# One causal convolution layer on a Trainium2 core: the input projection as seven block products instead of eight, with its sums on VectorE and a short convolution spread over three engines

## The chip, the core and the metric

The kernel runs on one core of a Trainium2 chip, in fp32 throughout. Time is device time in microseconds of one launch. Its engines are called here by what the profile calls them: PE (TensorE, the matrix engine), DVE (VectorE), ACT (ScalarE), POOL (GpSimd) and SP (the engine that issues most DMAs). PE multiplies a stationary block of weights with moving columns and writes into PSUM, eight banks of 512 fp32 columns for 128 partitions; DVE, ACT and POOL work on SBUF, and DVE and ACT also read and write PSUM. Each engine takes its instructions in order and stands at one whose operands are not ready.

## The reference

The input is x of 8192 tokens by 512 channels. A layer of the kind "long convolution with gates" is followed by a mixture of 32 x 4 small experts; each is added to its input and normalized. What matters here is the beginning:

```python
u = x @ W_in + b_in                          # 8192 x 1536
uc = _short_conv(u, short_w, short_b)        # 3 taps along the tokens, per channel
x0, x1, v = jnp.split(uc, 3, axis=-1)
v = v * x1
k = _gen_filter(x.shape[1], W1, b1, f1, W2, b2, f2, W3, b3)   # two sine layers, then 512 channels
v = _causal_fft_conv(v, k, filter_bias)      # the long convolution
y = v * x0
return y @ W_out + b_out
```

The filter k depends on the position alone: a 3-row table goes through two dense layers with a sine each, a third layer to 512 channels, and a decay by an exponential.

## The kernel before

The program has stages that follow each other: `project`, `convolve` (the long convolution as matmuls with tables of cosines and sines), and `experts`. Only `project` is touched. It has channels on the partitions and tokens along the columns. Between the stages three arrays lie in DRAM: x0, the gate (v * x1) and the taps (the filter k).

**The projection.** Sixteen blocks of 512 tokens, and in each four tiles of 128 channels. `projection(b, ct)` forms the tile's three outputs s = 0, 1, 2 (x0, x1 and v), each from four matmuls over 128 of the 512 input channels (L260, fp32, 128x512), in a PSUM bank of its own. All PSUM banks of the stage come from one pool of eight single banks.

**The short convolution.** For each s, ACT moves the bank to SBUF with the bias (L269, into `u`, which has two columns more for the last two tokens of the block before), and multiplies by the third tap (L271). DVE adds the second tap (L272) and the first (L277, or L283 in two halves for s = 0, whose result is stored in another order). POOL copies the two last columns to `carry` and back (L253, L286) and multiplies the outputs 1 and 2 (L288). SP stores x0 and the gate (256 KB each).

**The filter, riding along.** `rides` is a list of 16 filter steps and 32 tap groups, dealt out over the 64 (b, ct) pairs in order: behind each pair the loop issues as many as fall due. A filter step (`filter_1` or `filter_2`) is one 128x512 matmul (L209, L215) and a `sine`: seven DVE instructions (L197 to L202: a reduction of the argument in three steps with `n` and `a`, then a clamp) and ACT's sine (L203). A tap group (`some_taps`) has eight short matmuls into two banks (`pk`); for each bank ACT makes four 128x128 exponentials `ex` (L238), DVE adds the bias to give `kb` (L241), and POOL multiplies the two into `taps` (L245). A finished tile of taps (4 MB) is stored by SP.

**Order.** Tiles come from pools with a number of buffers for each tag (`bufs`); a new tile of a tag waits until the oldest one's readers are done. A scheduler of the build orders the instructions on each engine, and the waits follow from reads, writes and buffers. Tokens come in as `xt`, 1 MB for a block, with two buffers.

## Time and profile before

| | before |
|---|---|
| median of 3 runs | 2326.41 us (2322.28 to 2327.26) |
| profiled execution | 2320.76 us, its span 2319.0 us |
| mean granted PE clock | 0.969 |
| PE busy in the span | 2152.6 us (93%) |
| DVE, ACT, POOL busy | 1297.3 (56%), 823.7 (36%), 478.2 us (21%) |
| the projection's matmuls (L260) | 1536 records, 673.5 us busy |
| waits in the span's first 724 us before L260 | 4.8 us |

The slices of the page cut the span in 40 equal parts of 58 us; a digit is the busy share in tenths. The groups give, for a line of the code, an engine and the names of what is written and read, the count, the busy time, the mean of one in ns, and the time that the engine stood idle just before, with what ended most of it. An fp32 matmul of 512 columns leaves two records and two weight loads in this trace. The first stage takes the first 724 us, some twelve and a half slices.

### The profile page before, as it was taken

To read this page: it belongs to the slowest core of one execution; us is meant where nothing else is said; L and a number is where in the kernel's file an instruction comes from. 1 tells how busy PE (TensorE), PEld (TensorE's weight loads), DVE (VectorE), ACT (ScalarE), POOL (GpSimd) and SP (SyncE) were. 2 spreads that over 40 slices of the span, in tenths; PEclk is the share of its full clock that TensorE was granted. 3 is DMA by queue.
4 is the path that set the end of the run, shared out by engine and by line. 5 is a ranking of instruction groups with operands and counts; after the bars stand their busy time and mean duration, and the time that the engine had idled before them with its cause. 6 is when DMAs were issued, how large, how long until landed. Compare 5 with 4: busy or idle time off the path is not lost. (4 is left out here: it accounts for less than half of the span.)

```text
span 2319.0 us, 65860 instructions
## 1 busy us (share of the span) xinstructions
PE 2152.6 (93%) x29664; PEld 1474.7 (64%) x29664; DVE 1297.3 (56%) x1872; ACT 823.7 (36%) x1248; POOL 478.2 (21%) x583
## 2 busy tenths in 40 slices
PE   9999999999999999999999998889988999888765
PEld 3444444444446999999999998355555556555643
DVE  5677544554544553463463463456566666656647
ACT  4444555555553321231321221121343234224433
POOL 1111333333331340250250160211100100110000
PEclk9999999999999999999999999999998999899887
DMA  5222224232414655655564574526654754665373
GB/s 167 68 64 76 70 65 167 87 136 64 141 59 168 204 172 192 194 199 183 184 219 174 165 245 167 154 77 195 216 193 136 230 185 137 194 217 188 118 264 121
DMA packets 197057, 362.62 MB, mean 156 GB/s; under 512 B 79132, under 2 KB 118946, under 8 KB 193698
## 3 DMA queue, kind: packets, MB, share of 16 engines
q1 hardware_dynamic: 194472, 341.63, 45.2%
q10 hardware_dynamic: 2304, 16.78, 1.8%
q8 instruction: 233, 3.82, 0.7%
q14 instruction: 48, 0.39, 0.1%
HBM read 274.47 MB, written 83.89 MB: 155 GB/s over the span
## 5 line engine op out<-in xcount | busy, mean ns | idle before, releaser
L260 PE MATMUL pu<-xt,win 128*128 128x512 f32 x1536 | 673.5, 596 | 4.8 <-DMA xt<-in_xT 4.8
L260 PEld LDWEIGHTS pu<-xt,win 128*128 128x128 f32 x1536 | 289.2, 190 | 363.8 <-issue 355.0
L272 DVE SCALAR_TENSOR_TENSOR o<-u,chan_sb,o 128x512 f32<-128x512 f32 x192 | 144.8, 754 | 289.6 <-ACT o L271 270.6
L554 PE MATMUL po<-wout,yt 128*128 128x512 f32 x512 | 240.7, 614 | 19.4 <-DVE x L558 19.2
L383 PE MATMUL px<-place,tab 128*64 128x128 f32 x4096 | 227.6, 273 | 2.2 <-ACT place L366 1.4
L383 PEld LDWEIGHTS px<-place,tab 128*64 128x64 f32 x4096 | 226.0, 136 | 3.3 <-ACT place L366 2.1
L359 PE MATMUL pa<-c_in_sb,vk 128*64 128x128 f32 x4096 | 224.9, 273 | 2.3 <-ACT place L366 1.6
L359 PEld LDWEIGHTS pa<-c_in_sb,vk 128*64 128x64 f32 x4096 | 223.5, 137 | 3.9 <-ACT place L366 1.8
L552 POOL TENSOR_TENSOR xt<-xt,b_outb_sb 128x512 f32<-128x512 f32 x64 | 82.4, 1288 | 619.9 <-DMA xt<-in_x 581.1
L269 ACT ACTIVATE u<-pu,chan_sb 128x512 f32<-128x512 f32 x192 | 130.6, 680 | 182.8 <-PE pu L260 179.0
L405 POOL TENSOR_TENSOR place<-t,hs 128x256 f32<-128x256 f32 x132 | 94.8, 718 | 470.8 <-DVE hs L403 411.2
L554 PEld LDWEIGHTS po<-wout,yt 128*128 128x128 f32 x512 | 94.4, 194 | 130.1 <-issue 96.1
L717 ACT COPY si<-pi 128x1024 f32<-128x1024 f32 x96 | 93.0, 1012 | 196.6 <-PE pi L708 138.3
L271 ACT ACTIVATE o<-u,chan_sb 128x512 f32<-128x512 f32 x192 | 155.6, 812 | 6.5
L368 DVE COPY place<-pa 128x1024 f32<-128x1024 f32 x64 | 78.3, 1224 | 139.7 <-PE pa L359 135.1
L721 DVE STREAM_TRANSPOSE si<-si 128x2048 f32<-128x2048 f32 x48 | 108.1, 2290 | 85.0 <-ACT si L717 85.0
L366 ACT COPY place<-pa 128x1024 f32<-128x1024 f32 x64 | 64.7, 1012 | 251.8 <-PE pa L359 245.7
L416 PE MATMUL pz<-c_back_sb,place 64*128 64x128 f32 x2048 | 123.6, 284 | 14.8 <-POOL place L405 14.8
L238 ACT ACTIVATE ex<-delta_sb,negt_sb 128x128 f32<-128x128 f32 x256 | 87.6, 390 | 132.9 <-POOL taps L245 132.9
L416 PEld LDWEIGHTS pz<-c_back_sb,place 64*128 64x128 f32 x2048 | 122.8, 199 | 15.8 <-POOL place L405 15.8
L708 PE MATMUL pi<-f,h 32*32 32x128 f32 x6144 | 103.4, 291 | 30.2 <-issue 18.2
L398 ACT COPY hs<-px 128x512 f32<-128x512 f32 x132 | 75.5, 572 | 156.9 <-PE px L383 149.0
(86 smaller groups left out, 2655.9 us busy)
## 6 DMA issues: line engine op xcount, KB each, us to landing
f<-in_f SPq DMA_DIRECT2D x160, 512.0 KB, 5.1
tab<-in_c_mid SPq DMA_DIRECT2D x64, 512.0 KB, 3.8
place<-in_c_out SPq DMA_DIRECT2D x64, 512.0 KB, 5.0
x<-o SPq DMA_DIRECT2D x64, 256.0 KB, 2.4
gate<-gate SPq DMA_DIRECT2D x64, 256.0 KB, 2.6
taps<-taps SPq DMA_DIRECT2D x4, 4096.0 KB, 11.2
vk<-taps SPq DMA_DIRECT2D x32, 512.0 KB, 4.0
vk<-gate SPq DMA_DIRECT2D x32, 512.0 KB, 3.5
```

Source lines behind the costliest of these rows:

```text
L260: nc.tensor.matmul(pss[s], win[ct][:, k, s, :], xt[:, k, :], start=(k == 0), stop=(k == NCT - 1))
L269: nc.scalar.activation(u[:, s, 2:], pss[s], AF.Identity, bias=ch(0))
L271: nc.scalar.activation(o, u[:, s, 2:], AF.Identity, bias=ch(1), scale=ch(4))
L272: nc.vector.scalar_tensor_tensor(o, u[:, s, 1 : 1 + TB], ch(3), o, ALU.mult, ALU.add)
L359: nc.tensor.matmul(ps[r * 64 : (r + 1) * 64, c * N1 : (c + 1) * N1], vk[:, half * 8 + c, :], cin[:, r, :], start=True, stop=True,)
L383: nc.tensor.matmul(ps[h * 64 : (h + 1) * 64, j, :, r, :], tab[:, g % 2 * KC + j, r * 64 : (r + 1) * 64], both[:, :, g * KC + j, h * 64 : ( ...
L405: nc.gpsimd.tensor_tensor(o[:, 0], t[:, 0], hs[:, 1], ALU.subtract)
L416: nc.tensor.matmul(ps[:, h, c, :], spec[rows, r, c0 + c, :], cback[rows, r].rearrange("p q n -> p (q n)"), start=(r == 0), stop=(r == 1),)
L554: nc.tensor.matmul(ps, got["y"][:, ct, t % 2 * P : (t % 2 + 1) * P], wout[:, ct, :], start=(ct == 0), stop=(ct == NCT - 1),)
L708: nc.tensor.matmul(pss[r // 2][s * T : (s + 1) * T, col : col + P], b.h[rows, at + q, s, u * T : (u + 1) * T], f2[rows, q, s, :], start=Tr ...
L717: nc.scalar.copy(o, pss[rr].rearrange("p (r q d) -> p r d q", r=2, q=4))
L721: nc.vector.transpose(turned[:, d].rearrange("p d g -> p (d g)"), stage[:, d].rearrange("p d e -> p (d e)"),)
```

## The change

The projection takes double blocks of 1024 tokens and pairs of channel tiles m and m + 2, so that a "quad" (b, m, s) is a product of a 2 x 2 block matrix of weights (two channel tiles by two halves of the 512 input channels) with a 2 x 2 block matrix of tokens (two halves of the input channels by two runs of 512 tokens). Such a product takes eight block products when written out. The changed kernel forms it from seven, on sums of weight blocks and of token blocks. A block product is two fp32 128x512 matmuls (L317).

- *Sums of operands.* Four sums of weight blocks for each m at the start (L184 to L187, DVE for m = 0 and POOL for m = 1), and four differences of token tiles `t1` to `t4` for each double block (L208; on DVE for the first one, on POOL after that). `t1` has two buffers, the others one.
- *Sums of results.* p1 has a single bank and goes to SBUF by ACT (L327). The other six products fall in three bank pairs: p26, p75 and p43. DVE adds each pair of banks in one instruction of 1024 columns (L338, L350, L355), and once 512 columns (L351). The pairs come from a pool of two, so that p26 of a quad takes the pair that p75 of the quad before gives back, and so on in turn. The other four banks are a pool of single banks, for p1, the short convolution's halves (`o_`), the filter steps and the tap groups.
- *The short convolution* of a quad is issued in the middle of the next one: ACT multiplies by the first tap in SBUF (L372, 1024 columns) and by the third, with a combined bias, into a single PSUM bank (L379, 512 columns); DVE adds the second tap (L387, reads PSUM, writes SBUF); POOL adds the first (L397, or L401 for s = 0). For s = 1 quads after the first 27, DVE adds the first tap (L391) and ACT's part of it falls away. The bias of the projection enters by the combined bias; `carry` starts with minus the bias. POOL multiplies the gate (L411), 1024 columns at once.
- *Order.* PE's instructions keep the order in which they are written (`manual_schedule`); the other engines' are ordered by the scheduler. A quad has on PE: p1, p26, the rides that are due, p75, p43. The 16 filter steps fall in the first 27 quads, the 32 tap groups in the next 19. The outputs go in the order s = 1, 2, 0.
- *Loads.* The first weight block is loaded by ACT's queue. Tokens come as four tiles of 512 KB for a double block, from a tag with five buffers; the position rows for `filter_1` in eight loads.

The diff (empty lines left out):

```diff
--- before.py
+++ after.py
@@ -125,12 +125,18 @@
             for name in ("chan", "c_in", "c_back")
         }
         between = in_dram("x0", [P, L]), in_dram("gate", [P, P, N2]), in_dram("taps", [P, P, N2])
-        with tc.tile_pool(name="psum1", bufs=8, space=bass.MemoryType.PSUM) as psum:
+        with (
+            tc.tile_pool(name="psum1", bufs=4, space=bass.MemoryType.PSUM) as psum,
+            tc.tile_pool(name="psum0", bufs=2, space=bass.MemoryType.PSUM) as psum0,
+        ):
             def bank(name):
                 return psum.tile([P, 512], F32, tag="ps", name=name)
-            project(tc, i, bank, load, between, kept)
+            def pair(name):
+                return psum0.tile([P, 2, TB], F32, tag="pair", name=name)
+            project(tc, i, bank, pair, load, between, kept, pairs)
         with tc.tile_pool(
             name="psum2", bufs=4, space=bass.MemoryType.PSUM, reuse_waits="tile"
         ) as psum:
@@ -142,43 +148,80 @@
     experts(tc, i, load, ident, y_dram, out)
-def project(tc, i, bank, load, between, kept):
+def project(tc, i, bank, pair, load, between, kept, small):
     nc = tc.nc
     x0_dram, gate_dram, taps_dram = between
-    with tc.tile_pool(name="pr1", bufs=1) as hp, tc.tile_pool(name="pr2", bufs=2) as wk:
-        win = [hp.tile([P, NCT, 3, P], F32, tag=f"win{ct}", name=f"win{ct}") for ct in range(NCT)]
-        def load_win(ct):
+    with (
+        tc.tile_pool(name="pr1", bufs=1) as hp,
+        tc.tile_pool(name="pr2", bufs=2) as wk,
+        tc.manual_schedule(engines={nc.tensor.engine}),
+    ):
+        NP = NCT // 2
+        A11, A12, S3, A22, S1, S2, S4 = range(7)
+        win = [hp.tile([P, 7, 3, 2, P], F32, tag=f"win{m}", name=f"win{m}") for m in range(NP)]
+        def load_win(m, queue):
             come = i["W_in"].rearrange("(k p) (s t c) -> k t p s c", p=P, s=3, c=P)
+            for half in range(2):
+                for k in range(NCT):
+                    queue.dma_start(
+                        out=win[m][:, 2 * half + k // 2, :, k % 2, :], in_=come[k, m + NP * half]
+                    )
+        def sums_of_win(m, e):
+            w = win[m]
+            e.tensor_tensor(w[:, S1], w[:, S3], w[:, A22], ALU.add)
+            e.tensor_tensor(w[:, S2], w[:, S1], w[:, A11], ALU.subtract)
+            e.tensor_tensor(w[:, S4], w[:, A12], w[:, S2], ALU.subtract)
+            e.tensor_tensor(w[:, S3], w[:, A11], w[:, S3], ALU.subtract)
         def load_tokens(b):
-            xt = wk.tile([P, NCT, TB], F32, tag="xt", name=f"xt_{b}")
-            nc.sync.dma_start(
-                out=xt, in_=i["xT"][:, b * TB : (b + 1) * TB].rearrange("(k p) t -> p k t", p=P)
+            got = {}
+            for name, h, n in (("12", 0, 1), ("11", 0, 0), ("21", 1, 0), ("22", 1, 1)):
+                got[name] = xq = wk.tile([P, 2, TB], F32, tag="xq", name=f"xq{name}_{b}", bufs=5)
+                t0 = (2 * b + n) * TB
+                nc.sync.dma_start(
+                    out=xq,
+                    in_=i["xT"][2 * h * P : 2 * (h + 1) * P, t0 : t0 + TB].rearrange(
+                        "(k p) t -> p k t", p=P
+                    ),
+                )
+            return got
+        def sum_of_tokens(b, x, name, e):
+            a, c = {"1": ("12", "11"), "2": ("22", "t1"), "3": ("22", "12"), "4": ("21", "t2")}[name]
+            x["t" + name] = t = wk.tile(
+                [P, 2, TB], F32, tag=f"xs{name}", name=f"xs{name}_{b}", bufs=2 if name == "1" else 1
             )
-            return xt
-        xt = wk.tile([P, NCT, TB], F32, tag="xt", name="xt_0")
-        for k in range(NCT):
-            nc.sync.dma_start(
-                out=win[0][:, k],
-                in_=i["W_in"].rearrange("(k p) (s t c) -> k t p s c", p=P, s=3, c=P)[k, 0],
-            )
-            nc.sync.dma_start(out=xt[:, k], in_=i["xT"][k * P : (k + 1) * P, 0:TB])
-        pe = load(hp, "pe")
+            e.tensor_tensor(t, x[a], x[c], ALU.subtract)
+        load_win(0, nc.scalar)
...
+        load_win(1, nc.sync)
         w3 = load(hp, "W3p")
         b3 = load(hp, "b3b")
         negt = load(hp, "negt")
@@ -187,12 +230,22 @@
             nc.sync.dma_start(out=kept[name], in_=i[name])
         h2 = hp.tile([P, L // 2], F32, tag="h2", name="h2")
...
+        carry = hp.tile([P, 3, 2, NP, 2], F32, tag="carry", name="carry")
...
         def sine(dst, ps, layer, name):
...
+            a = small.tile([P, 512], F32, tag="t", name="a" + name)
+            n = small.tile([P, 512], F32, tag="hs", name="n" + name, bufs=3)
             b_ap, f_ap = bf[:, 2 * layer : 2 * layer + 1], bf[:, 2 * layer + 1 : 2 * layer + 2]
             nc.vector.tensor_scalar(a, ps, b_ap, f_ap, ALU.add, ALU.mult)
             nc.vector.tensor_scalar(n, a, 1.0 / (2 * math.pi), ROUND, ALU.mult, ALU.add)
@@ -205,8 +258,10 @@
         h1s = {}
         def filter_1(j):
+            pe = wk.tile([6, 512], F32, tag="pe", name=f"pe_{j}", bufs=1)
+            nc.sync.dma_start(out=pe, in_=i["pe"][:, bass.ts(j, 512)])
             ps = bank(f"pf1_{j}")
...
+            nc.tensor.matmul(ps, w1, pe, start=True, stop=True)
             h1s[j] = wk.tile([P, 512], F32, tag="h1", name=f"h1_{j}")
             sine(h1s[j], ps, 0, f"0_{j}")
@@ -232,8 +287,8 @@
                     )
             for half in range(2):
                 n2 = half * N2 // 2 + 4 * j
...
+                ex = small.tile([P, 4, P], F32, tag="t", name=f"ex_{ct}_{n2}")
+                kb = small.tile([P, 4, P], F32, tag="hs", name=f"kb_{ct}_{n2}", bufs=3)
                 for q in range(4):
                     nc.scalar.activation(
                         ex[:, q, :], delta[:, chans], AF.Exp, scale=negt[:, n2 + q : n2 + q + 1]
@@ -248,52 +303,119 @@
             if j == N2 // 8 - 1:
                 nc.sync.dma_start(out=taps_dram[ct], in_=taps.pop(ct))
...
+        class Quad:
+            def __init__(self, b, m, s, x):
+                self.b, self.m, self.s, self.x = b, m, s, x
+                self.nm = f"_{b}_{m}_{s}"
+                self.u = wk.tile([P, 2, 2 * TB + 2], F32, tag="u", name="u" + self.nm, bufs=3)
+            def product(self, ps, slot, tokens):
+                for k in range(2):
+                    nc.tensor.matmul(
+                        ps, win[self.m][:, slot, self.s, k, :], self.x[tokens][:, k, :],
+                        start=(k == 0), stop=(k == 1),
+                    )
+            def p1(self):
+                self.now = carry[:, self.s, :, self.m]
+                nc.scalar.copy(self.u[:, :, 0:2], self.now)
+                ps = bank("p1" + self.nm)
+                self.product(ps, A11, "11")
+                nc.scalar.copy(self.u[:, 0, 2 : 2 + TB], ps)
+            def p2(self):
+                self.pair = pair("p26" + self.nm)
+                self.product(self.pair[:, 0], A12, "21")
+            def p6(self):
+                self.product(self.pair[:, 1], S2, "t2")
+                c2 = self.u[:, 0, 2:].rearrange("p (n t) -> p n t", n=2)
+                c1 = self.u[:, 1, 2:].rearrange("p (n t) -> p n t", n=2)
+                nc.vector.tensor_tensor(c1, self.pair, c2[:, 0:1].to_broadcast([P, 2, TB]), ALU.add)
+            def the_others(self):
+                c2 = self.u[:, 0, 2:].rearrange("p (n t) -> p n t", n=2)
+                u2 = self.u[:, 1:2, 2 + TB :]
+                c21 = self.u[:, :, 2 : 2 + TB]
+                rows, _, run = c21.ap
+                ends = bass.AP(c21.tensor, c21.offset, [rows, [3 * TB + 2, 2], run])
+                ps = pair("p75" + self.nm)
+                self.product(ps[:, 0], S3, "t3")
+                self.product(ps[:, 1], S1, "t1")
+                nc.vector.tensor_tensor(ends, ps, u2.to_broadcast([P, 2, TB]), ALU.add)
+                nc.vector.tensor_tensor(c2[:, 1], ps[:, 1], c2[:, 0], ALU.add)
+                ps = pair("p43" + self.nm)
+                self.product(ps[:, 0], A22, "t4")
+                self.product(ps[:, 1], S4, "22")
+                nc.vector.tensor_tensor(ends, ps, ends, ALU.add)
+                nc.scalar.copy(self.now, self.u[:, :, 2 * TB : 2 * TB + 2])
+        gates = {}
+        def short_convolution(q, on_dve):
+            b, m, s = q.b, q.m, q.s
+            for half in range(2):
+                ct = m + NP * half
+                u = q.u[:, 1 - half]
+                at = s * NCT + ct
+                w = wk.tile([P, 2 * TB], F32, tag="w", name=f"w_{half}{q.nm}", bufs=5)
+                by_half = lambda v: v.rearrange("p (a h b) -> p h a b", h=2, b=N2 // 2)
+                if not on_dve:
+                    of = u[:, 0 : 2 * TB]
+                    nc.scalar.activation(
+                        w if s else w.rearrange("p (h a b) -> p h a b", h=2, b=N2 // 2),
+                        of if s else by_half(of), AF.Identity, scale=ch[:, at, 2:3],
+                    )
+                for n in range(2):
+                    t0 = n * TB
+                    ps = bank(f"o_{half}_{n}{q.nm}")
+                    nc.scalar.activation(
+                        ps, u[:, t0 + 2 : t0 + 2 + TB], AF.Identity,
+                        bias=bias[:, at : at + 1], scale=ch[:, at, 4:5],
+                    )
+                    if on_dve:
+                        o = ps
+                    else:
+                        o = wk.tile([P, TB], F32, tag="o", name=f"o_{half}_{n}{q.nm}", bufs=3)
                     nc.vector.scalar_tensor_tensor(
...
+                        o, u[:, t0 + 1 : t0 + 1 + TB], ch[:, at, 3:4], ps, ALU.mult, ALU.add
+                    )
+                    if on_dve:
+                        nc.vector.scalar_tensor_tensor(
+                            w[:, t0 : t0 + TB], u[:, t0 : t0 + TB], ch[:, at, 2:3], o,
+                            ALU.mult, ALU.add,
+                        )
+                    elif s:
+                        wn = w[:, t0 : t0 + TB]
+                        nc.gpsimd.tensor_tensor(wn, o, wn, ALU.add)
+                    else:
+                        a = TB // N2
+                        wn = w.rearrange("p (h a b) -> p h a b", h=2, b=N2 // 2)[:, :, n * a : (n + 1) * a]
+                        nc.gpsimd.tensor_tensor(wn, by_half(o), wn, ALU.add)
+                if s == 0:
...
+                elif s == 1:
+                    gates[half] = w
+                else:
+                    gate = gates.pop(half)
+                    nc.gpsimd.tensor_tensor(gate, gate, w, ALU.mult)
...
         rides = []
@@ -303,19 +425,60 @@
             if j:
                 rides += [(filter_2, j - 1)]
         rides += [(filter_2, nf - 1)]
+        n_filter = len(rides)
         rides += [(some_taps, ct, j) for ct in range(NCT) for j in range(N2 // 8)]
...
+        n_quads = NTB // 2 * NP * 3
+        filter_until, taps_until = n_quads * 9 // 16, n_quads - 2
+        def rides_until(j):
+            if j < filter_until:
+                return n_filter * (j + 1) // filter_until
+            return n_filter + (len(rides) - n_filter) * (j + 1 - filter_until) // (taps_until - filter_until)
+        sum_of_tokens(0, x, "1", nc.vector)
+        sums_of_win(0, nc.vector)
+        for name in "234":
+            sum_of_tokens(0, x, name, nc.vector)
+        quads = [Quad(0, 0, s, x) for s in (1, 2, 0)]
+        for q in quads:
+            q.p1()
+        for q in quads[:2]:
+            q.p2()
+        for q in quads[:2]:
+            q.p6()
+        nxt, done, before = None, 0, None
+        for j in range(n_quads):
+            b, r = divmod(j, 3 * NP)
+            m, s = r // 3, (1, 2, 0)[r % 3]
+            if r == 0 and b:
+                x, nxt = nxt, None
+            if j < 3:
+                q = quads[j]
+            else:
+                q = Quad(b, m, s, x)
+                q.p1()
+            if j >= 2:
+                q.p2()
+                q.p6()
+            if before:
+                short_convolution(before, before.s == 1 and j > filter_until)
+            if j == 1:
+                sums_of_win(1, nc.gpsimd)
+            for f, *args in rides[done : rides_until(j)]:
+                f(*args)
+            done = max(done, rides_until(j))
+            q.the_others()
+            before = q
+            if b + 1 < NTB // 2:
+                if r == 1:
+                    nxt = load_tokens(b + 1)
+                if r in (3, 4):
+                    sum_of_tokens(b + 1, nxt, "12"[r - 3], nc.gpsimd)
+                if r == 5:
+                    sum_of_tokens(b + 1, nxt, "3", nc.gpsimd)
+                    sum_of_tokens(b + 1, nxt, "4", nc.gpsimd)
+        short_convolution(before, False)
```

## The prediction

> **What bounds the kernel now.** I read the slices of the span first, then the groups of the first 724 us (the projection, function `project`), then windows inside it, then the timeline of one filter step. The chain that ended last lies wholly in the last stage and says nothing here. In the page (slices of 58 us; digits are tenths):

> ```profile
> PE   9999999999999999999999998889988999888765
> ...
> DVE  5677544554544553463463463456566666656647
> ACT  4444555555553321231321221121343234224433
> POOL 1111333333331340250250160211100100110000
> ...
> L272 DVE SCALAR_TENSOR_TENSOR o<-u,chan_sb,o 128x512 f32<-128x512 f32 x192 | 144.8, 754 | 289.6 <-ACT o L271 270.6
> ...
> L717 ACT COPY si<-pi 128x1024 f32<-128x1024 f32 x96 | 93.0, 1012 | 196.6 <-PE pi L708 138.3
> ```

> The twelve slices of the projection have TensorE full, VectorE half full, GpSimd at 1 and then 3 tenths. The groups of that stretch (busy us, mean ns | idle before, releaser):

> ```profile
> L260 PE MATMUL pu<-xt,win 128*128 128x512 f32 x1536 | 673.5, 596 | 4.8 <-DMA xt<-in_xT 4.8
> ...
> L271 ACT ACTIVATE o<-u,chan_sb 128x512 f32<-128x512 f32 x191 | 154.8, 812 | 6.5
> ...
> L245 POOL TENSOR_TENSOR taps<-kb,ex 128x512 f32<-128x512 f32 x64 | 95.2, 1489 | 58.0 <-DVE kb L241 54.2 <-DMA taps<-taps 3.8
> ...
> L288 POOL TENSOR_TENSOR gate<-o,o 128x512 f32<-128x512 f32 x63 | 82.0, 1302 | 80.2 <-DVE o L277 80.2
> ...
> L201 DVE SCALAR_TENSOR_TENSOR a<-n,a 128x512 f32<-128x512 f32 x48 | 48.3, 1007 | 1.6
> L241 DVE TENSOR_TENSOR kb<-pk,b3b_sb 128x512 f32<-128x512 f32 x64 | 43.7, 683 | 0.0
> L229 PE MATMUL pk<-W3p_sb,h 64*128 64x128 f32 x512 | 37.2, 285 | 0.0
> ```

> The projection's matmuls waited 4.8 us in all, for the first tokens: a pure TensorE bound. The 768 fp32 matmuls leave two records each, 0.43 us apart (the weight loads of the timeline below), so one costs 0.86 us. The windows (busy us and count of PE, PEld, DVE, ACT, POOL; clock; DMA share, GB/s) show a full clock that can't rise into idle time:

> ```profile
> 0.00:20.00 20.00, 15.17 (x31) 6.73 (x32) 1.88 (x4) 4.64 (x6) 1.21 (x10) 1.00 0.81 219
> ...
> 100.00:200.00 100.00, 100.00 (x232) 43.31 (x231) 74.28 (x113) 44.73 (x62) 18.26 (x28) 1.00 0.22 69
> ...
> 300.00:400.00 100.00, 100.00 (x325) 46.49 (x324) 47.86 (x75) 56.05 (x110) 36.24 (x41) 1.00 0.37 126
> ```

> **What it saves.** A "quad" (two channel tiles, 1024 tokens, one of three outputs) takes 7 products of two matmuls for 16 matmuls before. 48 quads: 672 matmuls for 768, 96 x 0.86 = 82.6 us. The work left to TensorE is 672 x 0.86 + 16 filter matmuls x 0.86 + 32 tap groups x 1.16 (37.2/32) = 577.9 + 13.8 + 37.2 = 629 us, against 711 before. Before ended at 724.5: 13 us of start. A bare quad takes 14 x 0.86 = 12.04.

> **What the quad puts on the others.** VectorE: three sums over bank pairs (L338, L350, L355) of 1024 columns and one of 512 (L351). Nearest rows, PSUM and SBUF operands: L738 (128x1024) 1.21 and L558 (128x512) 0.68. 3 x 1.21 + 0.69 = 4.3. The middle tap (L387) is four times L272's form, 0.75, = 3.0. Together 7.3 of 12.04. ScalarE: carries 0.4, p1 copy 0.57 (L398's row), two first taps of 1024 at 1.15 (L717 has 1.01 from PSUM; I add what L271 has over L269, 0.13), four taps into PSUM; no ScalarE write to PSUM was seen before, I take L271's 0.81 (ends 0.57 and 1.0): 6.5. GpSimd: four adds of the first tap (L397/L401) at L288's undisturbed 1.27 = 5.1; per two quads of s=2 in a block, two gates of 1024 each (L411), 2.34 by the slope of GpSimd rows (128x256 0.72, 128x512 1.27: 2.1 ns a column), = 4.7; four token sums of 2.34 a block (L208).

> [...]

> A plain quad is covered. With t = 0 at the end of the previous quad's last product: D (L355) to 1.4, carry 1.6, first tap 2.8, p1 copy 3.4, taps into PSUM 4.2 and 5.0, S1 5.0, S2 5.7, A (needs p26, 5.2) 6.9, S3 7.7, S4 8.5, B 10.0, C (L351) 10.7. The next p26 needs C's pair at 12.04 + 1.7: 3 us spare. So 0 for it. The costs lie where a quad has more:

> *Start.* The first quad needs four token tiles and a whole weight block with its sums, 3.7 MB at the window's 219 GB/s = 17 us; then five VectorE sums before the first p6 (two of 1024 at 1.2, three of 768 at 0.95, some 5 us). By then TensorE has done p1 x 3 and p2 x 2, 8.6 us: idle 22 with the first waits after it, for 13 before: **+9** (5 to 17).

> *Filter steps* (16, in the first 27 quads). VectorE gets L197–L202: 0.81 + 3 x 0.42 + 3 x 0.69 = 4.1 more, and they meet GpSimd:

> ```profile
> 154.20 0.42 DVE L199 TENSOR_SCALAR n<-n 128x512 f32<-128x512 f32 x1
> 154.36 1.38 POOL L288 TENSOR_TENSOR gate<-o,o 128x512 f32<-128x512 f32 x1 [2.66 <-DVE o L277]
> ...
> 154.65 2.36 DVE L201 SCALAR_TENSOR_TENSOR a<-n,a 128x512 f32<-128x512 f32 x2
> ```

> Two L201 took 2.36 beside a gate, 0.69 each otherwise (median; mean 1.007). [...] With GpSimd at 18% in that window, L201 lost 48 x 0.315 = 15 us; at the new 8.6/12.9 = 67% that is 56, 3.5 a step. [...]

> *Block ends* (7 times, every sixth quad). In the order of the built program GpSimd does there four adds, two gates and token sums 2, 3, 4 (7.0), then sum 1 of the block after next, which also waits for its loads, and only then the next quad's adds. 5.1 + 4.7 + 7.0 = 16.8 in 12.5: 4.3 late, in filter time 4 x 5 = 20 with the sum behind it. S4 waits for a buffer of three (L386), B and C queue behind it on VectorE, p26 waits for C, and sums 3 and 4 are themselves operands of p75 and p43. In the taps part GpSimd also has 4 products of 1.4 (L300): 22.4 in 14.4, 8 late: 3 x 9 = 27. **47** (20 to 70).

> *The other gate quad* of a block in the taps part: 5.1 + 4.7 + 5.6 = 15.4 in 14.4; tap products end behind gates, kb (three buffers) and the exponentials (two) wait for them, and the next quad's ScalarE and VectorE work queues behind these: 3 x 5 = **15** (0 to 21).

> *Tap groups' banks.* Only four single banks now serve p1, four conv halves and two or four tap tiles. The first pair needs S1 and S2's banks (5.7, p26 ended at 5.2), the second S3 and S4's: 8.5, its work due at 6.3. So 0.6 for a quad with one group (6), 2.1 with two (13): 31. In six of them the convolution's last tap is on VectorE, four L391 more, and a bank is free after two instructions, not one: +2 each, 12. **43** (25 to 60).

> *Loads and queues.* SP issues four token loads of 512 KB per double block for two of 1 MB, eight more of the position rows, half as many stores of twice the size; the first weight block moves to ScalarE's queue, ahead of its first copies, within the start. The bytes are the same and the DMA share is 0.2 to 0.4, so 0 by rate. In order they matter once: the loads of tiles 12 and 11 for sum 1 wait on SP until tiles of the old block are free (sum 3 and the last p43), behind x0 and gate stores; the row of a 1 MB load is 5.8 us. GpSimd stands in that wait with the next quad's adds behind it: it is in the block ends.

> *End.* D and the last convolution (7 us) hold banks that the next stage takes at 1.6 before: **+5** (3 to 7).

> Sum: stage 629 + 22 + 28 + 47 + 15 + 43 = 784; 784 − 724.5 + 5 = +64. On the profiled execution's 2320.8 us (span 2319.0) that is 2385; the median of the runs stands 5.6 above it, so **2391**. Its own range, ends of the terms not all together: 2345 to 2425.

> **Rivals.**
> *Hidden after all, faster.* One mechanism: GpSimd's backlog is taken up by the buffers (five w, three o) and doesn't reach p26. For it: 6-quad mean load in filter time is 6 x 5.1 + 9.4 + 9.4 = 49 of 75 us. Against: the token sums 3 and 4 have one buffer, and the chain S4–B–C has 3 us. It drops 28 + 47 + 15: stage 694, −26, 2300. It decides when waits after the start fall below 133 − 64 = 69 us; the banks alone cost 43. Chance 0.15.
> *GpSimd becomes the bound.* Its rows stretch (L245 mean 1.49, L288 up to 1.65 beside VectorE). [...] For it: the taps part has GpSimd at 80% already. Chance 0.20.
> *Only the load's distribution is milder*: banks and start as summed, block ends half, sine nil: 2391 − 23 − 28 = 2340. Chance 0.12, slower still.
> That the products don't fall is excluded: the built program has 672. No change needs 69 us of waits to within 5: 0.03.

> The forecast itself gets 0.50. Range for 8 in 10: 2300 to 2445, leaving out some of the fast case and the far end of the slow one. Against the 0.2% (5 us) that a measurement can tell: faster 0.15, same 0.03, slower 0.82.

> **What would show it.** In the profile after: 1344 matmul records for the products; the stage's end near 784; their idle time some 100 us, most of it released by VectorE L351, tap groups released by L387 and L391; GpSimd at 6 to 8 tenths in the slices of the stage; L251–L254 well above 0.7 us; later stages unchanged. I am wrong if p26's idle time is under 30 us (the buffers take it up), if ScalarE is what p26 or S1 waits for (a PSUM write above 1.0), or if the start's idle exceeds 35 us.

## The result

The changed kernel takes 2383.14 us, the median of four runs (2380.78 to 2391.63), beside 2326.75 us for the kernel before in the same comparison: 1.0253 times as long (95% interval 1.0224 to 1.0282). The profiled execution took 2381.39 us, its span is 2379.6 us. The forecast was 2391 us.

The page of the changed kernel, its slices (59 us each; digits are tenths) and the larger group of the projection's matmuls (busy us, mean ns of one | idle before, releaser):

```profile
PE   8899898898889899999999999789998999899775
...
DVE  5877777555555464364364364356566567666557
ACT  3344444554554332132232232012243134224333
POOL 4647555656464251052051051121100100110000
PEclk9999999989999999999999999999999999999888
...
L317 PE MATMUL p<-xs,win 128*128 128x512 f32 x768 | 365.8, 624 | 1.1 <-POOL xs L208 1.1
```

The first thirteen slices were full for TensorE before and are 8 and 9 tenths now. GpSimd went from 1 to 3 tenths up to 4 to 7. There are 768 + 576 = 1344 matmul records, so the saved products are gone as planned. But their mean went up from 596 to 624 ns. The groups of the span's first 800 us, which name more releasers, have the second group of products and the others that matter:

```profile
L317 PE MATMUL p<-xq,win 128*128 128x512 f32 x576 | 274.3, 623 | 48.3 <-issue 22.3 <-DVE u L351 19.5 <-DMA win<-in_W_in 6.5
...
L387 DVE SCALAR_TENSOR_TENSOR o<-u,chan_sb,o 128x512 f32<-128x512 f32 x192 | 138.3, 745 | 134.7 <-ACT o L379 122.6 <-POOL w L401 12.1
...
L411 POOL TENSOR_TENSOR w<-w,w 128x1024 f32<-128x1024 f32 x32 | 77.3, 2415 | 2.4
...
L284 PE MATMUL pk<-W3p_sb,h 64*128 64x128 f32 x512 | 56.7, 320 | 30.4 <-DVE o L387 19.3 <-DVE w L391 6.8 <-DVE kb L296 4.3
...
L254 DVE SCALAR_TENSOR_TENSOR a<-n,a 128x512 f32<-128x512 f32 x48 | 52.7, 1097 | 1.1
...
L296 DVE TENSOR_TENSOR kb<-pk,b3b_sb 128x512 f32<-128x512 f32 x64 | 41.6, 683 | 53.5 <-POOL taps L300 51.2 <-PE pk L284 2.3
...
L251 DVE TENSOR_SCALAR n<-a 128x512 f32<-128x512 f32 x16 | 21.3, 1328 | 0.6
...
L252 DVE TENSOR_SCALAR n<-n 128x512 f32<-128x512 f32 x16 | 16.7, 1043 | 0.6
```

The products stood idle 49 us, most of it for L351 or with no releaser named ("issue"). The tap groups wait on TensorE for the convolution's reads of their banks (L387, L391). VectorE itself stands 51 us before `kb`, for GpSimd's tap products (L300). And two of the sine's instructions take 2.5 to 3.2 times as long as they did: L251 is the old L198, L252 the old L199, which the groups of before give as

```profile
L198 DVE TENSOR_SCALAR n<-a 128x512 f32<-128x512 f32 x16 | 6.7, 420 | 0.0
L199 DVE TENSOR_SCALAR n<-n 128x512 f32<-128x512 f32 x16 | 6.7, 418 | 0.0
```

L254, the old L201, went from a mean of 1007 ns to 1097 only.

The last weight load of the projection is at 780.4 us, so the stage ends at some 781 us, for 724.5 before. What follows the stage took 2379.6 − 781.2 = 1598 us, for 1595 before. So all but some 4 us of the loss lies in the stage. Laid on the spacing of the weight loads, with the bare time of 12.04 us for a quad, 0.86 for a filter step and 1.16 for a tap group taken off, the stage's 152 us beyond its 629 us of work fall so:

| stretch (TensorE's quads, end of the last weight load) | lost, measured | lost, forecast |
|---|---|---|
| start, quads 0 to 2, to 53.9 us | 17 | 22 |
| filter part, quads 3 to 26, to 403.6 us | 48 | 28 + 20 = 48 |
| taps part, quads 27 to 45, to 756.4 us | 87 | 27 + 15 + 43 = 85 |
| last two quads | 0 | 0 |

A block end in the filter part, in the timeline of the changed kernel (start, duration; the wait before it in brackets). On TensorE, from 86.02 us on, 8 records of p75 of the block's last quad follow each other at 0.43 us, 8 of p43 and 4 of the next quad's p1, so p75 is done near 89.5 and p1 near 94.6. The next p26 cannot begin until L350 and L351 have given p75's bank pair back:

```profile
87.38 2.35 POOL L411 TENSOR_TENSOR w<-w,w 128x1024 f32<-128x1024 f32 x1
...
89.68 2.52 POOL L208 TENSOR_TENSOR xs<-xq,xs 128x1024 f32<-128x1024 f32 x1
90.04 2.45 DVE L252 TENSOR_SCALAR n<-n 128x512 f32<-128x512 f32 x1
92.17 3.11 POOL L397 TENSOR_TENSOR w<-o,w 128x512 f32<-128x512 f32 x2
92.52 3.30 DVE L254 SCALAR_TENSOR_TENSOR a<-n,a 128x512 f32<-128x512 f32 x2
95.36 2.67 POOL L411 TENSOR_TENSOR w<-w,w 128x1024 f32<-128x1024 f32 x1
95.75 1.21 DVE L350 TENSOR_TENSOR u<-p,u 128x1024 f32<-128x1024 f32 x1
96.88 1.69 DVE L254 SCALAR_TENSOR_TENSOR a<-n,a 128x512 f32<-128x512 f32 x1
...
98.50 0.68 DVE L351 TENSOR_TENSOR u<-p,u 128x512 f32<-128x512 f32 x1
...
99.28 3.42 PE L317 MATMUL p<-xq,win 128*128 128x512 f32 x4 [4.51 <-issue]
```

GpSimd works without a gap, and each of VectorE's sine steps ends 0.3 to 0.6 us after the GpSimd instruction beside it. L350 stands behind three of these instructions, L351 behind a fourth. L351 ends at 99.18, and TensorE goes on at 99.28. The profile names no releaser for that wait ("issue"), yet it ends with L351; it is one of six that make the 22.3 us of "issue" in the group above.

And one in the taps part of the same kernel:

```profile
456.96 2.35 POOL L411 TENSOR_TENSOR w<-w,w 128x1024 f32<-128x1024 f32 x1
459.26 2.51 POOL L300 TENSOR_TENSOR taps<-kb,ex 128x512 f32<-128x512 f32 x2
...
460.57 0.69 DVE L296 TENSOR_TENSOR kb<-pk,b3b_sb 128x512 f32<-128x512 f32 x1 [8.47 <-POOL taps L300]
460.57 2.52 ACT L293 ACTIVATE ex<-delta_sb,negt_sb 128x128 f32<-128x128 f32 x8 [10.04 <-POOL taps L300]
...
462.43 0.69 DVE L351 TENSOR_TENSOR u<-p,u 128x512 f32<-128x512 f32 x1
463.16 2.37 POOL L208 TENSOR_TENSOR xs<-xq,xq 128x1024 f32<-128x1024 f32 x1
463.22 1.96 PE L317 MATMUL p<-xq,win 128*128 128x512 f32 x4 [2.93 <-issue]
...
466.80 1.28 ACT L293 ACTIVATE ex<-delta_sb,negt_sb 128x128 f32<-128x128 f32 x4 [2.27 <-POOL taps L300]
...
470.41 1.45 DVE L387 SCALAR_TENSOR_TENSOR o<-u,chan_sb,o 128x512 f32<-128x512 f32 x2 [5.96 <-ACT o L379]
...
471.21 0.49 PE L284 MATMUL pk<-W3p_sb,h 64*128 64x128 f32 x2 [4.32 <-DVE o L387]
```

Here GpSimd's gate delays the tap product, VectorE stands 8.5 us at `kb` for a buffer, L351 comes late and p26 waits. Then ScalarE's last exponentials wait for a tap product behind a token sum, the convolution's ScalarE work behind them is late, so L387 is, and the next tap group waits 4.3 us for its bank.

### The profile page after: what moved, and what is told of

Same layout as the page of the kernel before. It is cut to its first block, busy times and chain, and to the rows that moved or that the text cites. A ratio compares the mean times of both kernels' runs of the same rounds, so it can differ in the third digit from the quotient of the medians.

```text
span 2379.6 us, 65562 instructions
## 1 busy us (share of the span) xinstructions
PE 2129.9 (90%) x29472; PEld 1464.9 (62%) x29472; DVE 1399.2 (59%) x1852; ACT 809.2 (34%) x1284; POOL 702.9 (30%) x618
## 5 line engine op out<-in xcount | busy, mean ns | idle before, releaser
L317 PE MATMUL p<-xs,win 128*128 128x512 f32 x768 | 365.8, 624 | 1.1 <-POOL xs L208 1.1
L317 PE MATMUL p<-xq,win 128*128 128x512 f32 x576 | 274.3, 623 | 48.3 <-issue 22.3
L317 PEld LDWEIGHTS p<-xs,win 128*128 128x128 f32 x768 | 152.5, 202 | 198.2 <-issue 187.0
L717 PE MATMUL po<-wout,yt 128*128 128x512 f32 x512 | 244.4, 622 | 23.8 <-DVE x L721 18.5
L317 PEld LDWEIGHTS p<-xq,win 128*128 128x128 f32 x576 | 111.3, 197 | 196.5 <-issue 182.2
L387 DVE SCALAR_TENSOR_TENSOR o<-u,chan_sb,o 128x512 f32<-128x512 f32 x192 | 138.3, 745 | 134.7 <-ACT o L379 122.6
L397 POOL TENSOR_TENSOR w<-o,w 128x512 f32<-128x512 f32 x100 | 128.0, 1302 | 197.5 <-DVE o L387 142.4
L717 PEld LDWEIGHTS po<-wout,yt 128*128 128x128 f32 x512 | 95.6, 196 | 136.5 <-issue 100.8
L529 ACT COPY place<-pa 128x1024 f32<-128x1024 f32 x64 | 64.8, 1012 | 253.8 <-PE pa L522 253.8
L884 DVE STREAM_TRANSPOSE si<-si 128x2048 f32<-128x2048 f32 x48 | 108.1, 2290 | 71.9 <-ACT si L880 71.9
L379 ACT ACTIVATE o<-u,bias,chan_sb 128x512 f32<-128x512 f32 x192 | 141.8, 770 | 0.0
L579 PEld LDWEIGHTS pz<-c_back_sb,place 64*128 64x128 f32 x2048 | 122.2, 198 | 15.4 <-POOL place L568 15.4
```

The lines of the kernel that those rows point to most:

```text
L317: nc.tensor.matmul(ps, win[self.m][:, slot, self.s, k, :], self.x[tokens][:, k, :], start=(k == 0), stop=(k == 1),)
L379: nc.scalar.activation(ps, u[:, t0 + 2 : t0 + 2 + TB], AF.Identity, bias=bias[:, at : at + 1], scale=ch[:, at, 4:5],)
L387: nc.vector.scalar_tensor_tensor(o, u[:, t0 + 1 : t0 + 1 + TB], ch[:, at, 3:4], ps, ALU.mult, ALU.add)
L397: nc.gpsimd.tensor_tensor(wn, o, wn, ALU.add)
L579: nc.tensor.matmul(ps[:, h, c, :], spec[rows, r, c0 + c, :], cback[rows, r].rearrange("p q n -> p (q n)"), start=(r == 0), stop=(r == 1),)
L717: nc.tensor.matmul(ps, got["y"][:, ct, t % 2 * P : (t % 2 + 1) * P], wout[:, ct, :], start=(ct == 0), stop=(ct == NCT - 1),)
```

## The experiments

All but the two versions with three edits change one thing in the changed kernel. The table gives the median, the ratio to the kernel before with its 95% interval (the changed kernel: 1.0253) and the projection's last weight load in the profile (the changed kernel: 780.4 us). The work after the stage, which only the next stage's wait for the last banks ties to it, took 1583 to 1599 us in these profiles. So the last column is the sharper one for what happens inside the stage; it comes from one profile of each version, and the medians bear out its larger differences, not those of a microsecond or two.

| version | median, us | ratio to before | last load, us |
|---|---|---|---|
| no token sums | 2343.80 | 1.0109 (1.0077 to 1.0141) | 757.6 |
| rides late | 2317.27 | 0.9979 (0.9965 to 0.9993) | 726.8 |
| token sums on VectorE | 2371.95 | 1.0219 (1.0192 to 1.0246) | 779.2 |
| first tap always on GpSimd | 2357.16 | 1.0156 (1.0131 to 1.0181) | 766.4 |
| three edits together | 2287.34 | 0.9855 (0.9831 to 0.9879) | 697.1 |
| no reduction in the sine | 2358.07 | 1.0169 (1.0136 to 1.0202) | 752.7 |
| no gates | 2338.20 | 1.0080 (1.0052 to 1.0108) | 740.7 |
| eight products | 2420.93 | 1.0437 (1.0407 to 1.0467) | 833.3 |
| waits filled | 2379.56 | 1.0262 (1.0232 to 1.0293) | 788.4 |
| three edits, gates on VectorE | 2286.84 | 0.9853 (0.9830 to 0.9877) | 697.7 |

### GpSimd's load: token sums and gates taken away

Without the token sums of the later blocks:

```diff
-                if r in (3, 4):
-                    sum_of_tokens(b + 1, nxt, "12"[r - 3], nc.gpsimd)
                 if r == 5:
-                    sum_of_tokens(b + 1, nxt, "3", nc.gpsimd)
-                    sum_of_tokens(b + 1, nxt, "4", nc.gpsimd)
+                    for n in "1234":
+                        nxt["t" + n] = x["t" + n]
```

> Leaves out the differences of token tiles after the first double block (all later blocks reuse those of the first); everything else as in the changed kernel. Theory (GpSimd is late at the block ends by its token sums, my term of 47 us): p26 in the first quads of a block no longer waits 4 to 5 us, so some 40 us of waits go, and the half-speed stretches of TensorE behind them too (six or seven of 1.7 us): 2383 - 40 - 11 = about 2332. Rival (what is late there are the two gates and the convolution's adds, and the sums only follow them): less than 15 us, 2368 or more.

The stage became 22.8 us shorter; the ratio fell by 1.4%, some 33 us. That is more than the rival allows (15) and less than the theory said (51). The waits at p26 fell from 53 to 36 us by the spacing of the loads, so two thirds of them don't need the sums.

Without the gates:

```diff
                 elif s == 1:
-                    gates[half] = w
-                else:
-                    gate = gates.pop(half)
-                    nc.gpsimd.tensor_tensor(gate, gate, w, ALU.mult)
+                elif s == 2:
+                    gate = w
```

(The empty branch for s = 1 goes with it.)

> Leaves out the product of the outputs 1 and 2 (output 2 is stored alone). Theory as in the prediction: at block ends and at the other gate quads GpSimd has 4.7 us less, of 47 + 15 us of waits some 40 go: 2383 - 40 = 2343, with the half-speed stretches 2333. If only the other gate quads depend on it (15 us): 2368. Rival (GpSimd's load isn't what the waits come from): 2378 or more.

The stage became 39.7 us shorter, as expected. The waits at p26 halved, to 27 us, and VectorE's wait before `kb` fell from 51.2 to 22.4 us. So GpSimd's lateness is a cause, and the gates are the larger part of it, the token sums the smaller. The rival is out. By stretches, without the sums the filter part lost 36 us for 48 and the taps part 76 for 87; without the gates 33 and 60. No run leaves out both, so the two figures need not add.

The sums moved to VectorE, rather than left out:

```diff
-                    sum_of_tokens(b + 1, nxt, "12"[r - 3], nc.gpsimd)
+                    sum_of_tokens(b + 1, nxt, "12"[r - 3], nc.vector)
```

(and sums 3 and 4 in the same way)

> The token differences of all blocks on VectorE, not on GpSimd; nothing else changes. Theory (GpSimd late at block ends): GpSimd is relieved of 9.7 us a block, VectorE takes 4 x 1.2 us a block and, with two SBUF operands, waits for GpSimd: some 15 to 30 us better than the changed kernel, 2353 to 2368. Rival (VectorE is the engine that is short): 2383 or more.

This was a miss for both: the ratio says some 8 us better, with intervals that overlap, and the stage in the profile hardly moved (1.2 us). p26 waited 20 us less, but p75, p43 and the tap groups more. On VectorE the two kinds of sum took 1.49 and 1.73 us in the mean in this version, though 1.21 to 1.22 in the changed kernel's first block, where no GpSimd instruction ran beside them. So these sums, with both operands in SBUF, seem to have been held up as the sine was in the changed kernel (L254 1.10 us in the mean, for 0.69 at its median). The engine with the room was not free of the one without.

### The banks

The rides come between p75 and p43, not between p26 and p75:

```diff
-            for f, *args in rides[done : rides_until(j)]:
-                f(*args)
-            done = max(done, rides_until(j))
-            q.the_others()
+            def ride():
+                nonlocal done
+                for f, *args in rides[done : rides_until(j)]:
+                    f(*args)
+                done = max(done, rides_until(j))
+
+            q.the_others(ride)
...
                 nc.vector.tensor_tensor(c2[:, 1], ps[:, 1], c2[:, 0], ALU.add)
+                ride()
                 ps = pair("p43" + self.nm)
```

> Filter steps and tap groups are issued between p75 and p43, not between p26 and p75; nothing else changes. Theory (the tap groups wait for the banks of S3 and S4 because they come too early, my term of 43 us): they come 3.4 us later, when S4's bank is free at t = 8.5, so most of the 53 us of tap waits in the profile goes: about 2340 to 2350. Rival (S3 and S4 are late themselves, behind GpSimd's adds, so the wait only moves to another product): above 2370.

It gave more than expected: the stage is 53.6 us shorter, and the program is slightly faster than before the change. The groups of this version, in its first 790 us (a line number after 351 is one higher than in the changed kernel):

```profile
L317 PE MATMUL p<-xs,win 128*128 128x512 f32 x768 | 366.8, 622 | 28.4 <-DVE u L356 18.6 <-DVE u L338 8.8 <-DVE xs L208 0.9
L317 PE MATMUL p<-xq,win 128*128 128x512 f32 x576 | 261.0, 602 | 8.5 <-DMA win<-in_W_in 6.4 <-DVE u L351 1.4 <-PE p L317 0.7
...
L284 PE MATMUL pk<-W3p_sb,h 64*128 64x128 f32 x512 | 44.9, 296 | 18.5 <-DVE o L388 14.4 <-DVE w L392 3.9
L296 DVE TENSOR_TENSOR kb<-pk,b3b_sb 128x512 f32<-128x512 f32 x64 | 41.3, 683 | 42.5 <-POOL taps L300 42.5
```

The waits for banks fell, by the spacing from 53 to 34 us: that is the expected part. The other part is p26: it waited 53 us in the changed kernel and 5 here, and L351 is nearly gone as a releaser. GpSimd has exactly the same work, and VectorE still waits 42.5 us for its tap products. But the sine and `kb` now stand behind L350 and L351 in VectorE's order, not in front of them, and a wait there holds up p75 and p43 instead (L356, the old L355), by 43 us together where it was 10. So the place of the rides did two things, and the second, that they put slow VectorE work ahead of the two sums that p26 waits for, was not in the prediction. In the sum it is smaller than it looks: of the 48 us that p26 no longer waits, 33 come back at p75 and p43, so 15 are gained there, beside 19 at the banks. The rest is 6 us at the start, and a slower clock less often (48 us at half clock in the stage, for 82).

The first tap always on GpSimd:

```diff
-                short_convolution(before, before.s == 1 and j > filter_until)
+                short_convolution(before, False)
```

> The convolution's first tap is added by GpSimd in all quads, also in the seven of the taps part where VectorE did it. Theory (a bank is free after one VectorE instruction, not two: my +12 us): up to 12 us better, less what GpSimd's four adds more cost in a quad with room for them: 2373 to 2381. Rival (GpSimd is the bound of the taps part): 5.1 us more in each of seven quads, 2395 or more.

The stage is 14.0 us shorter, the ratio 0.97% lower. The six quads with two groups and that tap on VectorE took 17.0 to 20.7 us, 112.9 together; now five of them take 16.0 to 16.3, like the two-group quads without it, and the six 100.5. So having that tap on VectorE cost 12.4 us in these quads, where 12 was summed, and GpSimd has room for the adds in just these quads. (The edit frees a bank after one instruction, but it also takes four instructions from VectorE in each quad; no run separates the two.) In all the gain, 14 us in the stage and some 23 by the ratio, is above the 2 to 10 expected. The rival, GpSimd as the bound of the whole taps part, is wrong.

### The sine

Without the reduction of the argument, five of the sine's seven VectorE instructions (the sine is then taken of the clamped, unreduced value):

```diff
-            nc.vector.tensor_scalar(n, a, 1.0 / (2 * math.pi), ROUND, ALU.mult, ALU.add)
-            nc.vector.tensor_scalar(n, n, ROUND, None, ALU.subtract)
-            for c in (C1, C2, C3):
-                nc.vector.scalar_tensor_tensor(a, n, -c, a, ALU.mult, ALU.add)
```

> [...] Theory (my term of 28 us for the filter steps, by the exclusion with GpSimd): 2383 - 28 = 2355, with the half-speed stretches behind those waits 2345. Rival (the filter steps are absorbed by the plain quads between them): 2375 or more.

The stage is 27.7 us shorter, the size of the forecast term, and 26.7 of it lie in the filter part, which loses 21 us for 48. The ratio's fall, 0.84% or 20 us, and the medians, 25 us, are a little smaller. The run takes away the instructions themselves, some 2.9 us a step by their undisturbed durations, together with what they lose beside GpSimd, so it sizes the term and doesn't show those losses alone.

### The number of products

```diff
                 self.product(ps[:, 1], S4, "22")
+                self.product(ps[:, 1], S4, "22")
```

> The last product of each quad is issued twice, so TensorE has the old number of matmuls (768) in the new structure; the output stays the same. If TensorE bound every quad the time would grow by the full 96 x 0.86 = 82.6 us, to 2466. Theory (a third of the quads wait for other engines, with TensorE idle 3 to 6 us at p26): the longer product hides in some waits, so that growth is 40 to 60 us: 2423 to 2443. Rival (saved products were worth little since others bind everywhere): below 2410.

The stage grew by 52.9 us and the ratio by 1.84%, some 43 us (the median lies 2 us under the range given). So of 82.6 us of work some 30 to 40 fell into waits, or were made up by the clock (58 us at half clock in the stage, for 82). Read the other way round: at this arrangement of the other engines, going from eight products to seven is worth 43 to 53 us, not 82.6.

### Filling the waits

```diff
                 ps = bank("p1" + self.nm)
+                if self.b and self.s == 1:
+                    for _ in range(3):
+                        nc.tensor.matmul(
+                            ps, win[self.m][:, A11, self.s, 0, :], self.x["11"][:, 0, :],
+                            start=True, stop=True,
+                        )
                 self.product(ps, A11, "11")
```

> The changed kernel with three more matmuls at the head of p1 in the first quad of each half block (14 quads: those where p26 waited 4 to 5 us); they write the bank that p1 then overwrites, so the output stays the same. 42 matmuls more, 36 us of TensorE work, in places where it stood still for some 50 us. Theory (a still TensorE is granted half the clock for the next 3.4 us, about 1.4 us lost behind each such wait): the wait is filled, p1 comes 2.6 us later and what hangs on it costs some 10 us, but the half-speed stretches of these quads go: 2378 to 2388, and in the profile fewer half-speed stretches in these quads. Rival (the clock isn't set by the idle time before it): 2392 or more, with as many half-speed stretches as before.

42 matmuls more, 36 us of work, and the time is that of the changed kernel within the intervals; the stage is 8.0 us longer. In the changed kernel p26 waited 3.5 to 5.4 us in nine of these fourteen quads. The windows of the taps part (busy us and count of PE, PEld, DVE, ACT, POOL; granted clock; DMA share, GB/s), first of the changed kernel:

```profile
404.00:757.00 353.00, 308.05 (x1046) 151.12 (x1045) 196.11 (x246) 176.53 (x413) 201.65 (x141) 0.92 0.30 99
```

and of this version:

```profile
404.00:757.00 353.00, 318.74 (x1093) 155.36 (x1091) 204.64 (x255) 183.97 (x420) 202.15 (x140) 0.97 0.29 94
```

The granted clock rose from 0.92 to 0.97 by having TensorE do more. In the whole stage the trace has 82 us at half clock in the changed kernel and 44 us here. The rival expected as many as before. Over the whole span the six executions of this version had a clock of 0.953 to 0.963, the four of the changed kernel 0.947 to 0.953, so the change isn't that of one profile alone.

### What is left to gain

The three edits together, rides late, first tap on GpSimd, and token sums 2 to 4 on VectorE (the last in this form, with sums 3 and 4 on VectorE as above):

```diff
-                    sum_of_tokens(b + 1, nxt, "12"[r - 3], nc.gpsimd)
+                    sum_of_tokens(b + 1, nxt, "12"[r - 3], nc.vector if r == 4 else nc.gpsimd)
```

> Rides between p75 and p43, the first tap always on GpSimd, and the token differences 2, 3 and 4 on VectorE (1 stays on GpSimd). Theory (three separate causes: banks asked for too early, VectorE's second tap on a bank, GpSimd late at block ends): the gains add in part, and the half-speed stretches that are left mostly go: 2317 less 20 to 35, 2282 to 2297, below the kernel before. Rival (one cause seen three times; after the rides are moved nothing is left to gain): 2310 to 2320.

2287.34 us, 1.45% faster than the kernel before (1.21 to 1.69). Its groups in the first 790 us:

```profile
L317 PE MATMUL p<-xs,win 128*128 128x512 f32 x768 | 356.7, 608 | 14.8 <-DVE u L356 8.8 <-DVE u L338 5.4 <-DVE xs L208 0.5
L317 PE MATMUL p<-xq,win 128*128 128x512 f32 x576 | 259.7, 600 | 7.9 <-DMA win<-in_W_in 6.0 <-issue 1.2 <-PE p L317 0.7
```

The stage ends 83 us sooner than in the changed kernel and 26 sooner than before the change; 17 us at half clock are left of 82. The rival, one cause seen three times, is out: alone the three gave 54, 14 and 1 us (the last with all four sums moved), 69 together. Which of them is worth more beside the others, no run tells. With the gates on VectorE as well:

```diff
-                    nc.gpsimd.tensor_tensor(gate, gate, w, ALU.mult)
+                    nc.vector.tensor_tensor(gate, gate, w, ALU.mult)
```

> As the version with three edits, and the gate product on VectorE, not GpSimd. Theory (what is left of the waits in the taps part is GpSimd late behind two gates): 4.7 us a gate quad go from GpSimd, 2.4 come to VectorE and wait for GpSimd at times: 2275 to 2285. Rival (VectorE is now the scarcer engine): 2290 or more.

No difference (0.9853 and 0.9855). The theory's figure was missed by 2 us and the rival's by 3. But the weight loads show two effects that cancel: the taps part became 7.6 us shorter (301.1 for 308.7), which fits the theory, and the filter part, where VectorE has the sine, 8.7 longer (325.2 for 316.5), which fits the rival. p26 waits again in it (22 us for 4), and p75 and p43 hardly. A kernel with the gates on VectorE in the taps part alone would be the next to try; none was run.

## Why the prediction was right, and where

**The sign and the size** were right: +64 us forecast, +56 measured. The work saved was as worked out (1344 records). The losses by stretch came within 5 us of the sums. That closeness is in part luck, as the parts below show: some were too large, and a cost that was left out, the clock, made up for them.

**Start.** 17 us for 22; the term was 5 too large.

**Filter steps: 28 us.** No run shows the 28 of the sum by itself; the run without the reduction gave 27.7 in its place, for the instructions and their losses together, so the size was right. The prediction took 3.5 us lost in a step beside GpSimd; against their undisturbed durations L251, L252, L254 and L255 lost 16 x 0.91 + 16 x 0.63 + 48 x 0.41 + 16 x 0.31 = 49 us, 3.1 a step. But the text expected all of it at L254, as in the trace of before: 15 us there were to grow to 56 with GpSimd's share, and they grew to 20. The other 30 of the 49 fell on instructions with one SBUF input, L251, L252 and L255. Before, none of these began beside a GpSimd instruction, and they took 0.42, 0.42 and 0.43 us. In the changed kernel 15, 7 and 4 of the 16 of each did, and 16 of the 48 L254; all 42 were held up, and ended 0.28 to 0.29 us (L254 0.55) after the GpSimd instruction. So the term came out right in part by luck. The instructions with a PSUM operand were not held up: 80 of the 192 L387 began beside a GpSimd instruction and 24 of the 48 L351, and all took 0.734 to 0.756 and 0.676 to 0.694 us.

**Block ends and the other gate quads: 47 + 15 us.** GpSimd's overload is shown: 22.8 us went with the sums, 39.7 with the gates. The split between the two was off: p26 also waited some 8 us in quads 9 and 21, in the middle of a block of the filter part, where the forecast had nothing, and leaving the gates out gave 15 us in that part. And a step of the chain is wrong. "S4 waits for a buffer of three, B and C queue behind it": VectorE waited for GpSimd before L387 only 12.1 us in all. In front of B and C stood, in the taps part, `kb` waiting for its buffer (51.2 us, a link that the prediction named only for the other gate quads), and, in the filter part, the sine held up beside GpSimd (L252 2.45 us for 0.42), as the two timelines show. The run with late rides shows that order mattered: p26's wait fell from 53 to 5 us with GpSimd's work unchanged, though p75 and p43 took 33 of it over. ScalarE, one of the signs of being wrong, wrote to PSUM in 0.77 us, not over 1.0. L387 did wait for it (122.6 us), as in the prediction's plain quad, where S1 follows the taps. The run with the first tap on GpSimd gives ScalarE more to do and is faster, but no run lightens it, so its part in the lateness stays open.

**Banks: 43 us.** The tap groups waited 53 us by the spacing. The two figures of it that can be read alone fit: two-group quads waited 2.0 (2.1 was said), those with a tap on VectorE 3.0 to 4.5 (4.1 was said), the slower clock taken off. The one-group quads, said to wait 0.6, waited up to 5.4, since they follow the gate quads and L387 is late there.

**End.** The next stage's matmuls waited 6.9 us for 2.3 before: +4.6 for the +5.

**Not in the sum: the clock.** "A full clock that can't rise into idle time" was true (1.00 in the windows of before), and it didn't look the other way. The stage spent 82 us at half clock; 65 neighbouring weight loads stand 0.80 to 0.87 us apart, not 0.43, and the first load of each such pair is slow itself (0.34 us for 0.19); 4 pairs did before, all at the start. That is some 28 us. So the waits alone were about 124 us, a fifth less than the 155 that were summed, and the slow clock made up the rest. Two of the signs to look for say the same: the products' idle time is 49 us in the profile, not some 100, and GpSimd stands at 4 to 7 tenths in the slices, not 6 to 8. That the total fits is luck to this extent.

**Rivals.** "GpSimd becomes the bound" did not come: its adds (L397) took 1.302 and the gate 2.415 us, close to the 1.27 and 2.34 used, and it can take four more adds in some quads. "Hidden" failed as its point of decision said: 135 us of loss after the start, some 110 without the slow clock, for 69 that it could bear. The milder mix had the sine at nothing; the run without the reduction says 27.

## What to carry over

When one engine is full and its work is cut, ask first in which order the next engine takes what the full one waits for. Here VectorE was busy 265 of 350 us in the filter part, and a few slow instructions were put ahead of two sums, in an in-order queue beside a busy GpSimd. Moving the rides 3.4 us later, with the same work on every engine, shortened the stage by 53.6 us, by this order, the banks, the start and the clock together, beside 82.6 us of TensorE work saved. A load that is averaged over a block says little where a queue of two or three buffers ties it to a single quad. And count a wait of TensorE once for itself and again for the slower clock behind it: here some 28 us behind 124 us of waits.

## What was not expected of the hardware

The granted clock fell to half behind most waits of 2.5 to 5.4 us: after the start the changed kernel's weight loads show 17 such waits, and 14 were followed by a stretch at half clock; those that were not had 2.9, 3.2 and 3.5 us. In the changed kernel's weight loads around the block end shown above:

```profile
93.31 0.19 PEld L317 LDWEIGHTS p<-xq,win 128*128 128x128 f32 x1 [0.24 <-issue]
93.74 0.19 PEld L317 LDWEIGHTS p<-xq,win 128*128 128x128 f32 x1 [0.24 <-issue]
99.25 0.30 PEld L317 LDWEIGHTS p<-xq,win 128*128 128x128 f32 x2 [5.31 <-issue]
99.93 0.34 PEld L317 LDWEIGHTS p<-xq,win 128*128 128x128 f32 x1 [0.39 <-issue]
100.79 0.34 PEld L317 LDWEIGHTS p<-xq,win 128*128 128x128 f32 x1 [0.52 <-issue]
101.64 0.34 PEld L317 LDWEIGHTS p<-xs,win 128*128 128x128 f32 x1 [0.52 <-issue]
102.49 0.34 PEld L317 LDWEIGHTS p<-xs,win 128*128 128x128 f32 x1 [0.52 <-issue]
103.20 0.19 PEld L317 LDWEIGHTS p<-xs,win 128*128 128x128 f32 x1 [0.37 <-issue]
```

```profile
429.61 0.96 PEld L284 LDWEIGHTS pk<-W3p_sb,h 64*128 64x128 f32 x14 [0.40 <-DVE w L391]
431.40 0.29 PEld L284 LDWEIGHTS pk<-W3p_sb,h 64*128 64x128 f32 x2 [0.83 <-DVE w L391]
432.66 0.96 PEld L284 LDWEIGHTS pk<-W3p_sb,h 64*128 64x128 f32 x14 [0.96 <-DVE kb L296]
...
434.42 0.34 PEld L317 LDWEIGHTS p<-xs,win 128*128 128x128 f32 x1 [0.38 <-issue]
435.27 0.34 PEld L317 LDWEIGHTS p<-xs,win 128*128 128x128 f32 x1 [0.52 <-issue]
```

The half clock came here after waits of 0.4 to 1.0 us; in the 3.4 us before it (430.7 to 434.1) TensorE was busy for 2.0. The tap groups of before, without such waits, had no half clock. Here the next loads came 0.85, 0.86, 0.85 and 0.71 us apart, for 0.43, so that these waits cost 1.6 us more than themselves. With the stage from 20 us on cut into the windows that these starts mark, 15 of the 16 windows in which TensorE was busy for less than half were followed by half clock, 5 of the 10 with 50 to 60%, and 4 of the 196 with more. So in this trace the half clock went with the share of work in a window, not with one long wait.
